# Expert lists loaded ahead of the first weights, four column strips for small last tiles, and the tail's products moved last in a mixture-of-experts kernel

## The chip, the cores and the metric

The kernel runs on one core of a Trainium2 chip. The metric is device time in microseconds (us) of one launch. TensorE (PE in the profile, with PEld for its weight loads) multiplies, VectorE (DVE) and ScalarE (ACT) work on SBUF and PSUM, GpSimd (POOL) issues the indirect transfers (gathers and scatters by a list of indices), and SyncE (SP) issues most of the plain transfers. All arithmetic is float32, and each float32 product leaves two matmul records in the trace.

## What is computed

```python
x = x + xattn(layernorm(x), ctx_2048, ...)      # 8 x 256 tokens of 512, 32 heads, 8 key groups
x = x + ffn(layernorm(x), ...)                  # mixture of experts over the 2048 tokens

def ffn(hidden):                                # T = 2048, H = 512
    logits = x @ gate_w.T                       # 32 experts
    w, sel = top 4 of them, softmax weights normalised to sum 1
    large = sum over chosen e of cw[t,e] * (silu(x @ Wg[e]) * (x @ Wu[e])) @ Wd[e]       # inner width 192
    small = the same with cWg, cWu, cWd of chunk e // 2                                  # inner width 128
    return large + 0.05 * small
```

The reference evaluates all experts for all tokens and masks with `cw`; the kernel evaluates only the chosen pairs, about 4 x 2048 of them.

## The kernel before, in words

**First stage (to about 470 us).** Attention runs over eight batches by a table of slots. Each finished tile of 128 tokens is normalised, its rows are written to `xn_all` in DRAM, its four experts per token are found, and POOL scatters one entry (token number, weight) per choice into `lists` in DRAM, four indirect transfers a tile (L546). The two most loaded experts so far are worked on "ahead" for the first tokens while attention ends.

**Second stage.** Experts are ranked by load on the chip, and rank r gets a fixed capacity `CAPS[r]` (352, 320 x3, 304 x4, 288 x4, 272 x5, 256 x2, 240 x6, 224 x3, 208, 192, 160, 128). The order of work is `RANKS`: first the two smallest (128 and 160), then 352, 320 and so on down to 192. A loop L1285 runs over these 32 shares; what overflows a capacity would go to a loop at the end (L1307), which has nothing to do here. For share i:

- `numbers(i)` (L1198) loads the expert's number and the start of its list into SP registers; for all but the first it is held behind the last weight load recorded so far.
- `fetch_list(i)` (L1209, `list_of` L978) loads the list from DRAM: one transfer of 8-byte entries on SP, and a second of 64 rows if the share's last tile is "few".
- `fetch_weights(i)` (L1218, `weights_of` L965) loads `wm` (1,280 KB) and `sm` (768 KB) on SP; for i = 1 and 2 the load of `wm` also waits until the gathers of i - 1 have landed. Four buffers of each.
- `fetch_tokens(i)` (L1222, `tokens_of` L988) gathers the rows, one indirect transfer on POOL for each 128 tokens; three buffers.
- `turned` (L1008) transposes rows on TensorE into `exT`, four chunks, which stand between the five products of the share before; `inner` (L1025) makes g, u, ug, gs and us (five products of four 128-row steps) and from them the three operands `a`, `at` (64 wide, the tail of the 192) and `b`.
- `down` (L1067) makes the second layer by tiles of 128 tokens, `py`, then evicts them (`evict`, ACT and DVE) and scatters them with add into `out` on POOL (L1091).

`tiles_of` (L999) sorts tiles: full ones by pairs ("first", "second"), a last tile of up to 64 tokens is "few". For a pair the 64-row tail products of the two tiles use the upper and lower half of TensorE's rows at once, and stand between the products of `a` and of `b` (L1121 to L1127). A few tile puts `a` on output partitions 0 to 63 and `b` on 64 to 127, so both run at once, and the two halves are added in the eviction, for which the list's weights are loaded a second time to partitions 64 to 127.

SP and POOL each take their instructions in program order. At the seam between the stages, L1261 to L1284, the order on SP is: number of share 0, `wm` 0, list start of share 0, `sm` 0, numbers of shares 1 and 2, lists 0, 1 and 2, weights 1, weights 2, list 3. A list can be loaded only when all scatters into `lists` have landed. On POOL it is: the last scatters into `lists`, gathers 0 and 1, the add of the first ahead expert (L1248), gathers 2, gathers 3, the add of the second, then the stores of share 0.

Of the kernel before, what the change touches and what calls it, by code (L numbers as in the profile page):

```python
# [10 lines left out]
F32 = mybir.dt.float32  # L11
# [3 lines left out]
ALU = mybir.AluOpType  # L15
AX = mybir.AxisListType

P = 128
B, S, E = 8, 256, 512
# [13 lines left out]
RANKS = [len(CAPS) - 1, len(CAPS) - 2] + list(range(len(CAPS) - 2))  # L33
SHARES = [CAPS[r] for r in RANKS]
NS = (max(CAPS) + P - 1) // P
HALF = P // 2
MAXT = B * S
NO_ONE = NS * P

# [25 lines left out]
def xattn_moe(ctx: ExitStack, tc, x, ctxT, wqT, wkT, wvT, wfcT, bfc, gateT, wx, ws, out):  # L65
# [6 lines left out]
    nc = tc.nc  # L72
# [6 lines left out]
    lists = nc.dram_tensor("lists", (NE * MAXT, 2), F32, kind="Internal").ap()  # L79
# [21 lines left out]
    def counting(name, n, step, per_partition, base=0):  # L101

        i = const.tile([P, n], I32, tag=f"{name}_i", name=f"{name}_i")
        nc.gpsimd.iota(i, [[step, n]], base=base, channel_multiplier=per_partition)
        f = const.tile([P, n], F32, tag=f"{name}_f", name=f"{name}_f")
        nc.vector.tensor_copy(f, i)
        return i, f

    token_i, _ = counting("token", NT, P, 1, NO_ONE)
    _, part_f = counting("part", 1, 0, 1)  # L110
    _, col_f = counting("col", P, 1, 0)
    iota_e = col_f[:, :NE]
    _, base_f = counting("base", NE, MAXT, 0)
# [32 lines left out]
    with ExitStack() as att:  # L146
# [530 lines left out]
        def ahead(n):  # L677
# [45 lines left out]
            def gated_tail():  # L723
                st = steps["sg"][:HALF, 1, :]
                act.activation(st, sums["ug"][HALF:], AF.Silu)
                for j in range(2):
                    tok = slice(j * P, (j + 1) * P)
                    dve.tensor_tensor(
                        at[j * HALF : (j + 1) * HALF, tok], st[:, tok], sums["ug"][:HALF, tok],
                        ALU.mult,  # L730
                    )
# [8 lines left out]
            def second():  # L740
# [4 lines left out]
                for j in range(2):  # L745
                    part = slice(j * HALF, (j + 1) * HALF)
                    pe.matmul(py[j], lhsT=at[part, toks[j]], rhs=wt[part], start=False, stop=False)
# [119 lines left out]
        for s in range(16 * B + LAG + 6):  # L867
            k, i = divmod(s, 8)
# [7 lines left out]
            b, slot = divmod(s, 16)  # L876
# [7 lines left out]
            if s == 10:  # L884

                hold(nc.sync.dma_start(
                    out=lists.rearrange("(e n) c -> e n c", e=NE)[:, :NO_ONE, :], in_=no_one
                ))
                hold(nc.sync.dma_start(
                    out=lists.rearrange("(e n) c -> e n c", e=NE)[:, NO_ONE : NO_ONE + S, :],  # L890
                    in_=no_one[:, :S, :],
                ))
                hold(nc.sync.dma_start(
                    out=xn_all[:NO_ONE, :].rearrange("(j p) r -> p j r", p=P),
                    in_=nothing.unsqueeze(1).to_broadcast([P, NS, E]),
# [28 lines left out]
        count, _, at_rank = ranked("count", first_ones["took"])()  # L924
# [33 lines left out]
    m2 = ctx.enter_context(tc.tile_pool(name="m2", bufs=2, reuse_waits="tile"))  # L958
# [19 lines left out]
    def list_of(entries, n, ns, few=False):  # L978

        li = ls.tile([P, NS + 1, 2], F32, tag="li", name=f"li_{n}")  # L980
        nc.sync.dma_start(out=li[:, :ns, :], in_=entries.rearrange("(j p) c -> p j c", p=P))
        if few:
            nc.sync.dma_start(out=li[HALF:, NS, :], in_=entries[(ns - 1) * P :][:HALF])
        return li
# [14 lines left out]
    def tiles_of(w):  # L999

        sizes = [min(P, w - i) for i in range(0, w, P)]
        lots = ["few" if m <= HALF and len(sizes) > 1 else "" for m in sizes]
        full = lots.count("")
        for j in range(full - full % 2):
            lots[j] = "second" if j % 2 else "first"
        return list(zip(sizes, lots))
# [60 lines left out]
    def down(n, acts, wm, sm, li, weight, w):  # L1067

        a, at, b = acts
        wa, wt, wb = wm[:, 3 * E : 4 * E], wm[:, 4 * E :], sm[:, 2 * E :]  # L1070
        stores = []
        py = {}
        tiles = tiles_of(w)

        def evict(j):
            m, lot = tiles[j]
            y = m6.tile([P, E], F32, tag="y", name=f"y_{n}_{j}")
            if lot == "few":
                y2 = m2.tile([HALF, E], F32, tag="y2", name=f"y2_{n}_{j}")
                nc.scalar.activation(  # L1080
                    y2[:m], py[j][HALF : HALF + m], AF.Copy, scale=li[HALF : HALF + m, NS, 1:2]
                )
                nc.vector.scalar_tensor_tensor(
                    y[:m], py[j][:m], weight(j)[:m], y2[:m], ALU.mult, ALU.add
                )
            elif j % 2:
                nc.vector.tensor_scalar(y[:m], py[j][:m], weight(j)[:m], None, ALU.mult)  # L1087
            else:
                nc.scalar.activation(y[:m], py[j][:m], AF.Copy, scale=weight(j)[:m])  # L1089
            stores.append(  # L1090
                nc.gpsimd.indirect_dma_start(  # L1091
                    out=out,
                    out_offset=bass.IndirectOffsetOnAxis(
                        ap=li[:m, j, 0:1].bitcast(I32), axis=0
                    ),
                    in_=y[:m],
                    in_offset=None,
                    compute_op=ALU.add,
                )
            )  # L1100
        for j, (m, lot) in enumerate(tiles):
            tok = slice(j * P, (j + 1) * P)
            py[j] = ps_y.tile([P, E], F32, tag="py", name=f"py_{n}_{j}")
            if lot == "first":
                continue
            if lot == "few":


                tok = slice(j * P, j * P + HALF)
                nc.tensor.matmul(py[j][:HALF], lhsT=a[:, tok], rhs=wa, start=True, stop=False)  # L1110
                nc.tensor.matmul(py[j][HALF:], lhsT=b[:, tok], rhs=wb, start=True, stop=False)
                for i in range(2):
                    cols = slice(i * (E // 2), (i + 1) * (E // 2))
                    nc.tensor.matmul(
                        py[j][i * HALF : (i + 1) * HALF, cols],
                        lhsT=at[:HALF, tok], rhs=wt[:HALF, cols], start=False, stop=True,
                    )
            else:
                pair = [j - 1, j] if lot == "second" else [j]
                toks = [slice(i * P, (i + 1) * P) for i in pair]  # L1120
                for i, s in zip(pair, toks):  # L1121
                    nc.tensor.matmul(py[i], lhsT=a[:, s], rhs=wa, start=True, stop=False)
                for h, (i, s) in enumerate(zip(pair, toks)):
                    half = slice(h * HALF, (h + 1) * HALF) if len(pair) > 1 else slice(0, P)
                    nc.tensor.matmul(py[i], lhsT=at[half, s], rhs=wt[half], start=False, stop=False)
                for i, s in zip(pair, toks):
                    nc.tensor.matmul(py[i], lhsT=b[:, s], rhs=wb, start=False, stop=True)  # L1127
            for i in [j - 1, j] if lot == "second" else [j]:
                evict(i)
        return stores  # L1130
# [63 lines left out]
    held = {}  # L1194

    loads = []

    def numbers(i):  # L1198


        with tc.issue_after(loads[-1].ins) if i else nullcontext():
            held["expert", i] = nc.sync.value_load(
                order[0:1, RANKS[i] : RANKS[i] + 1], min_val=0, max_val=NE - 1
            )
            held["row", i] = nc.sync.value_load(
                begin[0:1, RANKS[i] : RANKS[i] + 1], min_val=0, max_val=NE * MAXT - NS * P
            )

    def fetch_list(i):  # L1209
        if i < NE:  # L1210
            if i > 2:
                numbers(i)
            held["list", i] = list_of(
                lists[bass.ds(held["row", i], ns_of[i] * P), :], i, ns_of[i],
                tiles_of(SHARES[i])[-1][1] == "few",
            )

    def fetch_weights(i):  # L1218
        if i < NE:
            held["weights", i] = weights_of(held["expert", i], i, gathers.get(i - 1) if i < 3 else None)  # L1220

    def fetch_tokens(i):  # L1222
        if i < NE:
            held["tokens", i] = tokens_of(held["list", i], i, ns_of[i])
# [17 lines left out]
    def behind(instruction):  # L1242
        return tc.issue_after(instruction.ins)
# [14 lines left out]
        ])  # L1258


    numbers(0)  # L1261
    fetch_weights(0)
    for i in range(1, 3):
        numbers(i)
    for i in range(3):
        fetch_list(i)
    fetch_tokens(0)
    fetch_weights(1)
    fetch_tokens(1)
    fetch_weights(2)  # L1270
# [14 lines left out]
    for i in range(NE):  # L1285
# [13 lines left out]
        li = held["list", i]  # L1299
# [7 lines left out]
    with tc.For_i(0, n_extra, 1) as i:  # L1307
        at = line.rearrange("o n c -> o (n c)")
# [4 lines left out]
        li = list_of(lists[bass.ds(row_r, P), :], "l", 1)  # L1313
# [4 lines left out]
        weight = m1.tile([P, 1], F32, tag="weight", name="weight")  # L1318
# [72 lines left out]
```

## Time and profile before

| | us |
|---|---|
| median of 3 runs | 1021.63 (1018.51 to 1031.36) |
| the profiled execution, its own device time | 1017.57 |
| its span, first to last instruction | 1015.4 |
| PE busy | 969.8 |
| DVE, ACT, POOL busy | 410.4, 318.2, 320.6 |
| mean granted TensorE clock | 0.983 |
| first g product of share 0, 1, 2, 3 starts | 497.77, 510.51, 523.52, 544.60 |
| last matmul ends | about 1001 |

By fortieths of the span, PE is at nine tenths or more nearly everywhere, and the row of the moved bytes shows two different halves: below 70 GB/s in most of attention, about 200 GB/s in the experts. Between them lies a short stretch, about 476 to 530 us, in which weights, lists, gathers and scatters of the first shares meet. Times inside the span are given from its start. "Landing" of a transfer is the time at which the trace records its completion.

### The profile page before, as it was taken

To read this page: it belongs to the slowest core of one execution; us is meant where nothing else is said; L and a number is where in the kernel's file an instruction comes from. 1 tells how busy PE (TensorE), PEld (TensorE's weight loads), DVE (VectorE), ACT (ScalarE), POOL (GpSimd) and SP (SyncE) were. 2 spreads that over 40 slices of the span, in tenths; PEclk is the share of its full clock that TensorE was granted. 3 is DMA by queue.
4 is the path that set the end of the run, shared out by engine and by line. 5 is a ranking of instruction groups with operands and counts; after the bars stand their busy time and mean duration, and the time that the engine had idled before them with its cause. 6 is when DMAs were issued, how large, how long until landed. Compare 5 with 4: busy or idle time off the path is not lost. (4 is left out here: it accounts for less than half of the span.)

```text
span 1015.4 us, 13821 instructions
## 1 busy us (share of the span) xinstructions
PE 969.8 (96%) x5068; PEld 594.2 (59%) x5068; DVE 410.4 (40%) x940; ACT 318.2 (31%) x561; POOL 320.6 (32%) x333
## 2 busy tenths in 40 slices
PE   5899999999999999899999999999999999999994
PEld 3445555556565654448665565565657567777773
DVE  4645676667666657535122221222222222122221
ACT  2255554545454544352121111222212111111110
POOL 4200131312222113233336534435343434433322
PEclk9799999999999999999899999999999999999997
DMA  6111010101010000503799876776867577777722
GB/s 219 46 36 65 32 53 33 55 32 34 24 41 12 33 12 33 219 32 92 209 376 190 210 228 176 200 197 180 232 172 223 155 228 229 227 222 213 219 37 33
DMA packets 57510, 133.49 MB, mean 131 GB/s; under 512 B 20737, under 2 KB 26114, under 8 KB 53218
## 3 DMA queue, kind: packets, MB, share of 16 engines
q1 hardware_dynamic: 28050, 79.18, 22.7%
q0 software_dynamic: 18976, 40.25, 19.0%
q10 hardware_dynamic: 10416, 13.18, 3.7%
q8 instruction: 40, 0.66, 0.3%
q14 instruction: 28, 0.23, 0.1%
HBM read 104.76 MB, written 27.56 MB: 130 GB/s over the span
## 5 line engine op out<-in xcount | busy, mean ns | idle before, releaser
L51 DVE TENSOR_REDUCE mx<-sc 128x4 f32<-128x1024 f32 x128 | 156.5, 1223 | 82.2 <-PE st L51 68.5
L51 ACT ACTIVATE pT<-st 128x1024 f32<-128x1024 f32 x128 | 131.0, 1024 | 134.5 <-PE st L51 130.1
L51 PE MATMUL sc<-kT,qT 32*128 32x512 f32 x512 | 146.1, 651 | 9.2 <-DVE mx L51 8.3
L991 POOL DMA_INDIRECT rows<-xn_all,li x80 | 78.7, 983 | 241.1 <-DMA li<-lists 62.2
L51 PE MATMUL st<-qT,k 32*128 32x512 f32 x512 | 144.3, 639 | 3.5 <-DMA qT<-mT 3.5
L1091 POOL DMA_INDIRECT out_dram<-y,li x80 | 122.5, 1531 | 73.7 <-ACT y L1089 45.2
L546 POOL DMA_INDIRECT lists<-ent,slot_i x64 | 62.4, 975 | 117.4 <-DVE slot_i L51 95.1
L1089 ACT ACTIVATE y<-py,li 128x512 f32<-128x512 f32 (+1 forms) x33 | 22.7, 687 | 163.8 <-PE py L1127 163.8
L1087 DVE TENSOR_SCALAR y<-py,li 128x512 f32<-128x512 f32 (+3 forms) x29 | 21.8, 751 | 121.4 <-PE py L1127 121.4
L1021 DVE COPY exT<-ept 128x384 f32<-128x384 f32 (+2 forms) x64 | 31.4, 490 | 94.8 <-PE ept L1015 89.1
L51 PEld LDWEIGHTS sc<-kT,qT 32*128 32x128 f32 x512 | 38.7, 186 | 49.0 <-DVE mx L51 26.4
L51 PE MATMUL pmq<-xT,wq_sb 128*128 128x256 f32 x256 | 63.8, 392 | 1.4 <-ACT xT L51 1.4
L51 PEld LDWEIGHTS pmq<-xT,wq_sb 128*128 128x128 f32 x256 | 46.0, 189 | 30.1 <-issue 23.5
L51 PE MATMUL po<-pT,va 128*32 128x512 f32 x512 | 63.1, 610 | 0.1
L51 PE MATMUL pmf<-wfc_sb,oT 128*128 128x256 f32 x256 | 63.0, 391 | 0.2 <-ACT oT L51 0.2
L1035 PE MATMUL pu_g<-exT,wm 128*128 128x240 f32 (+10 forms) x248 | 62.7, 395 | 0.0
L51 PEld LDWEIGHTS pmf<-wfc_sb,oT 128*128 128x128 f32 x256 | 46.2, 189 | 26.8 <-issue 15.2
L1127 PE MATMUL py<-sm,b 128*128 128x512 f32 x124 | 61.6, 617 | 0.0
L1035 PE MATMUL pu_us<-exT,sm 128*128 128x240 f32 (+10 forms) x248 | 60.6, 387 | 0.0
L1035 PE MATMUL pu_u<-exT,wm 128*128 128x240 f32 (+10 forms) x248 | 60.6, 387 | 0.0
L1035 PE MATMUL pu_ug<-exT,wm 128*128 128x240 f32 (+10 forms) x248 | 60.6, 387 | 0.0
L1035 PE MATMUL pu_gs<-exT,sm 128*128 128x240 f32 (+10 forms) x248 | 60.6, 387 | 0.0
(246 smaller groups left out, 1332.8 us busy)
## 6 DMA issues: line engine op xcount, KB each, us to landing
wm<-in_wx_dram SPq DMA_DIRECT2D x32, 1280.0 KB
sm<-in_ws_dram SPq DMA_DIRECT2D x32, 768.0 KB
acc<-in_x_dram SPq DMA_DIRECT2D x16, 256.0 KB
ctx<-in_ctxT_dram ACTq DMA_DIRECT2D x8, 512.0 KB
out_dram<-acc ACTq DMA_DIRECT2D x16, 256.0 KB
xn_all<-row ACTq DMA_DIRECT2D x16, 256.0 KB
rows<-xn_all,li POOLq DMA_INDIRECT x80, 3.7
out_dram<-y,li POOLq DMA_INDIRECT x80, 8.5
```

Source lines behind the costliest of these rows:

```text
L51: this = instruction(*args, **kwargs)
L546: nc.gpsimd.indirect_dma_start(out=list_views[TOPK * t + k], out_offset=bass.IndirectOffsetOnAxis(ap=slot_i[:, k : k + 1], axis=0), in_=en ...
L991: gathers[n] = nc.gpsimd.indirect_dma_start(out=rows[:, j, :], out_offset=None, in_=xn_all, in_offset=bass.IndirectOffsetOnAxis(ap=li[:, j ...
L1021: nc.vector.tensor_copy(xT[:, kc, : ns * P], pt[:, : ns * P])
L1035: tensor.matmul(pu[:, :w], lhsT=cols(kc), rhs=xT[:, kc, :w], start=(kc == 0), stop=(kc == KC - 1),)
L1087: nc.vector.tensor_scalar(y[:m], py[j][:m], weight(j)[:m], None, ALU.mult)
L1089: nc.scalar.activation(y[:m], py[j][:m], AF.Copy, scale=weight(j)[:m])
L1091: nc.gpsimd.indirect_dma_start(out=out, out_offset=bass.IndirectOffsetOnAxis(ap=li[:m, j, 0:1].bitcast(I32), axis=0), in_=y[:m], in_offset ...
L1127: nc.tensor.matmul(py[i], lhsT=b[:, s], rhs=wb, start=False, stop=True)
```

## The change

```diff
-HALF = P // 2
+HALF, QUARTER = P // 2, P // 4
...
-        lots = ["few" if m <= HALF and len(sizes) > 1 else "" for m in sizes]
+        lots = [
+            "" if m > HALF or len(sizes) == 1 else "few" if m > QUARTER else "very few"
+            for m in sizes
+        ]
...
                 nc.vector.scalar_tensor_tensor(
                     y[:m], py[j][:m], weight(j)[:m], y2[:m], ALU.mult, ALU.add
                 )
+            elif lot == "very few":
+                y2 = m2.tile([QUARTER, E], F32, tag="y2", name=f"y2_{n}_{j}")
+                for q in range(4):
+                    copy = nc.vector.tensor_copy if q % 2 else nc.scalar.copy
+                    copy(y2[:m, q * P : (q + 1) * P], py[j][q * QUARTER :][:m, :P])
+                nc.vector.tensor_scalar(y[:m], y2[:m], weight(j)[:m], None, ALU.mult)
...
+            elif lot == "very few":
+
+                tok = slice(j * P, j * P + QUARTER)
+                for u, w2, of in ((a, wa, P), (b, wb, P), (at, wt, HALF)):
+                    for q in range(4):
+                        nc.tensor.matmul(
+                            py[j][q * QUARTER : (q + 1) * QUARTER, :P],
+                            lhsT=u[:of, tok], rhs=w2[:of, q * P : (q + 1) * P],
+                            start=u is a, stop=u is at,
+                        )
             else:
                 pair = [j - 1, j] if lot == "second" else [j]
                 toks = [slice(i * P, (i + 1) * P) for i in pair]
                 for i, s in zip(pair, toks):
                     nc.tensor.matmul(py[i], lhsT=a[:, s], rhs=wa, start=True, stop=False)
+                for i, s in zip(pair, toks):
+                    nc.tensor.matmul(py[i], lhsT=b[:, s], rhs=wb, start=False, stop=False)
                 for h, (i, s) in enumerate(zip(pair, toks)):
                     half = slice(h * HALF, (h + 1) * HALF) if len(pair) > 1 else slice(0, P)
-                    nc.tensor.matmul(py[i], lhsT=at[half, s], rhs=wt[half], start=False, stop=False)
-                for i, s in zip(pair, toks):
-                    nc.tensor.matmul(py[i], lhsT=b[:, s], rhs=wb, start=False, stop=True)
+                    nc.tensor.matmul(py[i], lhsT=at[half, s], rhs=wt[half], start=False, stop=True)
...
-        with tc.issue_after(loads[-1].ins) if i else nullcontext():
+        with tc.issue_after(loads[-1].ins) if i > 2 else nullcontext():
...
-    numbers(0)
-    fetch_weights(0)
-    for i in range(1, 3):
+    for i in range(3):
         numbers(i)
-    for i in range(3):
         fetch_list(i)
     fetch_tokens(0)
+    with behind(held["lists", 2]):
+        fetch_weights(0)
     fetch_weights(1)
```

Three things are done. On SP the numbers and lists of shares 0, 1 and 2 now come first, and `wm` 0 and `sm` 0 behind them; the order on POOL stays. A last tile of up to 32 tokens becomes "very few": its 512 output columns are cut into four strips of 128, and strip q is written to output partitions 32q to 32q + 31, so that four products of 32 weight columns can stand side by side in TensorE; the strips are put together by two ACT and two DVE copies, and DVE multiplies by the weights. This holds for ten shares: 160, 288 (four) and 272 (five). For them the second list transfer is no longer made. In full tiles the tail's product now comes after that of `b`.

More of the change, by code (lines that the diff above doesn't have):

```diff
@@ L980, in list_of @@
         li = ls.tile([P, NS + 1, 2], F32, tag="li", name=f"li_{n}")
-        nc.sync.dma_start(out=li[:, :ns, :], in_=entries.rearrange("(j p) c -> p j c", p=P))
+        held["lists", n] = nc.sync.dma_start(
+            out=li[:, :ns, :], in_=entries.rearrange("(j p) c -> p j c", p=P)
+        )
         if few:
@@ L1117, in down @@
                     )
+            elif lot == "very few":
[6 more added lines that the diff above has]
+                            start=u is a, stop=u is at,
+                        )
             else:
```

## The prediction, made before the changed kernel ran

> **What bounds the kernel now.** I read the page's busy times, then the windows by stage, then the timeline of PE in one expert and at the seam, then SP's waits. The first lines say where time can be won.
>
> ```profile
> PE 969.8 (96%) x5068; PEld 594.2 (59%) x5068; DVE 410.4 (40%) x940; ACT 318.2 (31%) x561; POOL 320.6 (32%) x333
> ...
> 496.00:500.00 4.00, 2.20 (x15) 1.42 (x12) 1.24 (x3) 1.12 (x4) 3.39 (x3) 0.99 0.94 327
> 500.00:506.00 6.00, 5.33 (x25) 5.33 (x26) 1.26 (x4) 0.65 (x2) 2.24 (x3) 0.50 1.05 332
> 506.00:512.00 6.00, 5.88 (x31) 4.22 (x29) 0.35 (x2) 1.48 (x4) 0.00 (x0) 0.94 1.01 393
> 512.00:514.00 2.00, 0.57 (x3) 0.38 (x4) 0.00 (x0) 0.10 (x1) 0.00 (x0) 1.00 1.13 426
> 514.00:530.00 16.00, 16.00 (x82) 10.96 (x82) 3.86 (x9) 3.87 (x8) 6.28 (x6) 1.00 1.05 373
> ```
>
> The columns are length, PE, PEld, DVE, ACT, POOL, then granted clock, DMA share, GB/s. PE is the bound nearly everywhere; in the windows from 520 to 1000 us it is busy 480 of 480. The exception is the seam: PE half idle at 496 to 500, then half the clock for 6 us, idle again at 512 to 514. From 497 to 530 the DMA share is about 1.
>
> ```profile
> 500.67 0.47 PE L51 MATMUL ept<-ident,rows 128*128 128x128 f32 x1 [1.65 <-DMA rows<-xn_all,li]
> 500.94 1.91 PE L51 MATMUL pu_u<-exT,wm 128*128 128x128 f32 x8
> ...
> 507.04 1.06 PE L51 MATMUL pu_us<-exT,sm 128*128 128x128 f32 x8
> ...
> 512.83 0.33 PE L1015 MATMUL ept<-ident,rows 128*128 128x128 f32 x1 [0.95 <-DMA rows<-xn_all,li]
> 513.76 0.33 PE L1015 MATMUL ept<-ident,rows 128*128 128x128 f32 x1 [0.60 <-DMA rows<-xn_all,li]
> ...
> SPq L981 <- DMA lists<-ent,slot_i: 8.2, 1, 8.2
> ```
>
> PE waits for gathered rows; the same eight matmuls take 1.91 us at half clock and 1.06 at full. Behind that stands SP, which waits 8.2 us for the scatters into `lists`: the last is issued at 479.39 and lands at 488.83, because `wm` 0 and `sm` 0 (2.1 MB, issued at 476.20 and 477.78) are in the way. The scatters at 444 to 455, with no weights beside them, land 2.4 to 3.8 us after their start.
>
> ```profile
> 804.37 1.88 PE L1122 MATMUL py<-wm,a 128*128 128x512 f32 x4
> 806.18 1.13 PE L1125 MATMUL py<-wm,t 64*128 64x512 f32 x4
> 807.24 1.98 PE L1127 MATMUL py<-sm,b 128*128 128x512 f32 x4
> 809.15 0.64 PE L1110 MATMUL py<-wm,a 128*64 128x512 f32 x1
> ...
> 810.16 0.65 PE L1114 MATMUL py<-wm,t 64*64 64x256 f32 x4
> 810.74 0.73 PE L1035 MATMUL pu_g<-exT,wm 128*128 128x272 f32 x2
> ```
>
> This is the second layer of a 272 share. A record of 512 columns steps by 0.429 us (804.370, 804.799). From the last `a` record, 805.657, to the first tail record is 0.523: a change of the array's tiling costs 0.094. Going back to 128*128 also shows the first weight load: the first `b` step is 0.533, so 0.104 more. Records of the two halves (806.180, 806.187) or of four strips (`po` at 442.214, 442.220, 442.227, 442.234) start together.
>
> **Tail last.** For a pair the order tail, `b` became `b`, tail. Followed by a small tile (320 x3, 304 x4, 288 x4, 272 x5: 16 shares), tail to `b` (0.094 + 0.104) disappears and nothing new comes, since the small tile's change was there after `b`: 16 x 0.198 = 3.2 us. Followed by 128*128 work, g or the lone third tile of 352 (13 shares), the same 0.198 returns before it: 0. Lone tiles are 128*128 throughout: 0. What `b` loses is its cover: DVE finishes it at 805.08, and the last `a` ends at 806.09, 1.0 us later, against 0.19 for the weight load. In a lone tile it is 996.97 against 997.21, still just enough; cover gone, it would cost some 0.1 us in each of three shares. The pair's first eviction starts 0.9 us later; the next user of its PSUM buffer comes some 12 us later: 0.
>
> **Four strips.** Before, from the end of `b` (809.06) to g with its bare first load (810.74 + 0.104) is 1.78 us: two steps of 0.429, two of 0.213, the rest changes and first loads. After, six passes of 128 columns, 0.107 each (0.429/4, four strips at once), two first loads of 32 columns (0.027 in `po`: 0.453 against 0.427), three changes and g's load: 0.094 + 0.134 + 3 x 0.107 + 0.094 + 0.134 + 0.107 + 0.094 + 0.104 = 1.08. Saved 0.70 a tile; nine shares after the seam: 6.3 us. [...] `po` shows four strips for the price of one (16 records, 1.92 us, where 4 x 0.429 = 1.72). [...] I take the row, it is the same instruction form; bounds 0.8 saved and 1.2 lost a tile. The eviction: ACT and DVE copies by the 128x128 `exT` copies (0.27 and 0.28, two each) and a DVE multiply from SBUF (0.54, `row`), 1.1 us, against 0.68 + 0.74 before; nothing on PE waits for it (ACT and DVE are 20 to 24% busy there): 0. Ten list transfers of 64 rows fewer: SP and DMA, hidden from share 3 on: 0.
>
> **Lists first.** SP: six register loads and their checks (475.2 to 480.4 before, inside the 8.2 us wait) stay hidden. Then SP waits for the last scatter, now about 483 (479.39 + 3.5); behind this wait stand three list loads, then `wm` 0 and `sm` 0. List 0 goes at 483.0, not 489.09; `wm` 0 at about 485.1, not 476.20; it is needed at 497.77, and two megabytes take 6.4 to 9 us (`wm` 1 and `sm` 1: 496.3 to 505.3 beside gathers), so 495: in time, 2 to 3 us of cover for `wm`, more for `sm`. POOL follows the list by 6.1 us: gathers 0 at 485.6, not 491.69, the ahead adds at 489.4 (their operands are ready at 487.4), gathers 2 at 493.2. PE still ends the ahead work at 496.3. Rows 1 now land near 494 and are there: the 1.65 us wait and the half clock go, and us of share 0 starts at 502.3 (steps of 0.89 + 0.22) instead of 507.04: 4.7 us.
>
> What is late next: rows 2 (22.0 us from gather 0 to the landing at 513.72; 485.6 + 22 + 1 for sharing with `wm` 0 = 508.6, wanted at 507), and then rows 3. List 3 stands on SP's queue behind weights 0, 1, 2, now 6.3 MB from 486.4 instead of 4.2 MB from 496.3. At the 0.257 MB/us of before (496.3 to 512.6) that is 510.9, list 3 1.3 us later, 512.2 against 513.9. Rows 3 landed at 526.11 as PE wanted them (525.99), so they now land 2.1 earlier, 3.3 if the queue speeds up when POOL's part is over. PE is there at about 520 and waits some 3 us. So the seam gives 2.1 to 3.3, not 4.7, and perhaps a half clock: after 3.5 us idle (426.6 to 430.15) the clock was 0.58 over 431 to 435, 1.7 us lost; at 500 to 506 gaps of 1 to 2 us cost 3 us. [...] I take 1.2: 1.5 us.
>
> **Sum.** 3.2 + 6.3 + 1.5 = 11.0 us off the profiled execution's 1017.57 (span 1015.4 and 2.2 around it): 1006.6. The median, 1021.63, is 4.1 above that execution; I add it: 1010.7.
>
> **The rivals.**
> 1. Rows 3 come in time and the seam gives about 5: 1007. For it: POOL's part ends earlier, so SP's queue may run faster; against it, the DMA share of 1 up to 530.
> 2. The seam gives nothing or loses 2 (weights 0 late, or 3 us of half clock): 1012 to 1014.
> 3. Slower: narrow strips do not overlap. Then six passes cost 4 x 0.107 each, a tile 3.0 us, 9 x 1.2 = 11 lost against 4.7 won: 1028. It decides from 0.31 us a pass, where a tile costs 2.3. For it: weights change at every pass and a new load is due every 0.027 us. Against it: loads of `po` start 0.007 us apart.
> 4. The change does not do what it says: the scheduler could undo the orders; but the built orders of SP and PE show them, so only the timing is open.
>
> **Chances.** Main case 0.5; rival 1 0.2; rival 2 0.22; rival 3 and other losses 0.08. The range 1003 to 1018 leaves out rival 3 and the ends of run to run spread. More than 2% faster (under 1001.2) needs rival 1 and more than I can find: 0.05. Beyond 2% slower (over 1042.1): 0.02. Within 2%, about what a measurement here can tell from no change: 0.93.
>
> **What would show it.** List 0 issued near 483 and gathers 0 near 485.6; no wait at the second row transpose, clock 1.0 at 500 to 506; a wait of about 3 us before the first transpose of rows 3 near 520; 272 shares shorter by 0.9 us, 240 shares unchanged; strips starting within 0.03 us of each other. It is wrong if PE waits for `wm` 0, if strips follow each other by 0.1 us, or if PE waits before `b`.

## The result, and the profile after

The changed kernel takes 1011.7 us in the median of 19 runs (1008.14 to 1020.72), where the kernel before, run beside it, takes 1021.57. The ratio is 0.9892, with a 95% interval of 0.9863 to 0.9920 (the ratios here are estimated over the single runs; the quotient of the medians is 0.9903). That is within 2%, and 1 us above the forecast of 1010.7. In most kernels some runs lie 5 to 13 us over the median, at a mean granted clock of 0.968 to 0.975 where the others have 0.978 to 0.987, and the medians include them. The profiled execution took 1009.71 us, with a span of 1007.6. PE's part of the page:

```profile
PE 961.1 (95%) x5228; PEld 595.6 (59%) x5228; DVE 413.9 (41%) x960; ACT 316.1 (31%) x571; POOL 321.2 (32%) x333
```

PE is busy 8.7 us less than before, with 160 instructions more (the strips). DVE has 3.5 us more, and the lengths of the shares below show no wait for it. The seam, by the same windows as before (length, PE, PEld, DVE, ACT, POOL, granted clock, DMA share, GB/s):

```profile
496.00:500.00 4.00, 4.00 (x17) 2.50 (x15) 0.42 (x1) 0.38 (x1) 3.08 (x4) 1.00 1.06 319
500.00:506.00 6.00, 5.17 (x28) 3.16 (x28) 1.51 (x4) 1.50 (x4) 0.83 (x1) 1.00 1.04 371
506.00:512.00 6.00, 6.00 (x42) 4.80 (x41) 1.34 (x5) 1.24 (x4) 0.00 (x0) 1.00 1.00 415
512.00:514.00 2.00, 2.00 (x15) 1.76 (x14) 0.05 (x1) 0.99 (x2) 0.00 (x0) 1.00 1.09 407
514.00:530.00 16.00, 14.12 (x90) 9.87 (x89) 3.60 (x10) 3.12 (x8) 6.03 (x5) 1.00 1.06 374
```

The half clock at 500 to 506 is gone, and so are the waits for rows 1 and 2. That is not yet the work of the lists: PE's ahead work ended 6.5 us later than in the profile of before (the first transpose of rows 0 is at 502.85), so the rows had more time to come. Of these 6.5 us, 2.1 lie before PE counts the last tokens (472.19 and 474.31), ahead of all that the change touches. Another 1.9 us are lost at 520, where `b` of the second expert came late. So the g of the fourth expert starts at 545.91, where it started at 544.60: within this one pair of profiles the seam gave nothing, or 0.8 us if both are counted from the last tokens. Nearly the whole gain lies behind it. SP waits for the scatters into `lists` only for 2.1 us now:

```profile
SPq L981 <- DMA lists<-ent,slot_i: 2.1, 1, 2.1
```

The length of this wait also depends on when SP comes to it: it is 3.4 to 8.2 us in the six profiles below with the weights first and 1.7 to 5.1 in the four with the lists of three shares first. What the edit is for is seen better from POOL's last scatter into `lists` to the first gather of rows 0, before and after:

```profile
479.39 0.96 POOL L546 DMA_INDIRECT lists<-ent,slot_i  x1 [0.30 <-issue]
491.69 0.98 POOL L991 DMA_INDIRECT rows<-xn_all,li  x1 [11.34 <-DMA li<-lists]
...
481.51 0.96 POOL L546 DMA_INDIRECT lists<-ent,slot_i  x1 [0.30 <-issue]
489.07 0.98 POOL L993 DMA_INDIRECT rows<-xn_all,li  x1 [6.61 <-DMA li<-lists]
```

The second layer of a 272 share, to be set beside the lines of before (timeline of PE: start, busy time, line, operation):

```profile
798.28 1.88 PE L1143 MATMUL py<-wm,a 128*128 128x512 f32 x4
800.00 1.88 PE L1145 MATMUL py<-sm,b 128*128 128x512 f32 x4
801.81 1.13 PE L1148 MATMUL py<-wm,t 64*128 64x512 f32 x4
802.87 0.43 PE L1134 MATMUL py<-wm,a 128*32 128x128 f32 x8
803.11 0.40 PE L1134 MATMUL py<-sm,b 128*32 128x128 f32 x8
803.44 0.42 PE L1134 MATMUL py<-wm,t 64*32 64x128 f32 x8
803.80 0.72 PE L1040 MATMUL pu_g<-exT,wm 128*128 128x272 f32 x2
```

`b` follows `a` without a break (records 0.429 apart, 799.572 to 800.001): no change of tiling and no bare load stands between them. The small tile takes 0.93 us (802.87 to 803.80), where it took 1.59 (809.15 to 810.74). From one g to the next, shares have these lengths:

| share | before | changed | difference |
|---|---|---|---|
| 320 (the first; the two others) | 19.07; 18.56 | 18.87; 18.36 | 0.20 |
| 304 | 18.03 | 17.83 | 0.20 |
| 288 | 17.50 | 16.64 | 0.86 |
| 272 | 16.96 | 16.10 | 0.86 |
| 352, the second 256, 240 | 21.07, 14.21, 13.67 | 21.07, 14.21, 13.67 | 0 |

Sixteen shares at 0.20 and nine at 0.66 more make 9.1 us. The whole stretch agrees: from the g of the fourth expert to the end of the last matmul it is 456.08 us before and 446.97 after. (The first 256 share goes from 14.31 to 14.21, and the last share gets 0.10 longer: the bare first load of g now falls one share later.)

### The profile page after: what moved, and what is told of

Same layout as the page of the kernel before. It is cut to its first block, busy times and chain, and to the rows that moved or that the text cites. A ratio compares the mean times of both kernels' runs of the same rounds, so it can differ in the third digit from the quotient of the medians.

```text
span 1007.6 us, 14090 instructions
## 1 busy us (share of the span) xinstructions
PE 961.1 (95%) x5228; PEld 595.6 (59%) x5228; DVE 413.9 (41%) x960; ACT 316.1 (31%) x571; POOL 321.2 (32%) x333
## 5 line engine op out<-in xcount | busy, mean ns | idle before, releaser
L1145 PE MATMUL py<-sm,b 128*128 128x512 f32 x124 | 58.7, 593 | 1.9 <-DVE b L1068 1.9
```

## The experiments

**One part at a time.** The first three kernels carry one part of the change each, the fourth the strips and the tail without the lists. The edits stand against the kernel before; "..." marks what is left out of them.

Lists only:

```
-        with tc.issue_after(loads[-1].ins) if i else nullcontext():
+        with tc.issue_after(loads[-1].ins) if i > 2 else nullcontext():
...
-    numbers(0)
-    fetch_weights(0)
-    for i in range(1, 3):
-        numbers(i)
     for i in range(3):
+        numbers(i)
         fetch_list(i)
     fetch_tokens(0)
+    with behind(held["lists", 2]):
+        fetch_weights(0)
```

> Only the first three lists load ahead of the weights; strips and tail as before. My sum: 1.5 us off, ratio 0.9985 (some 1020.1 where before is 1021.6), with list 0 issued near 483 to 486 instead of 489.1 and rows 1 there when PE wants them. Rival 1 (the seam gives its full 5 us): ratio 0.995. Rival 2 (the seam gives nothing or loses 2): ratio 1.000 to 1.002. If the new gaps of PE between 477 and 484 that the changed kernel's profile shows come from this part, they are here too, and the ahead work ends near 503; if they come from the run, or from the tail or strips, they are gone and it ends near 496.

Strips only (with the eviction of the diff above):

```
+            elif lot == "very few":
+                tok = slice(j * P, j * P + QUARTER)
+                for u, w2, of in ((a, wa, P), (b, wb, P), (at, wt, HALF)):
+                    for q in range(4):
+                        nc.tensor.matmul(
+                            py[j][q * QUARTER : (q + 1) * QUARTER, :P],
+                            lhsT=u[:of, tok], rhs=w2[:of, q * P : (q + 1) * P],
...
```

> Only the four strips of columns for last tiles of up to 32 tokens. My sum: nine shares (288 x4, 272 x5) shorter by 0.70 us each, 6.3 us off, ratio 0.9938; 320 and 304 unchanged. [...] If the strips gained only by coming after a tail that is last (the changing of the array's tiling counted twice in my steps), less than 0.5 each.

Tail only:

```
+                for i, s in zip(pair, toks):
+                    nc.tensor.matmul(py[i], lhsT=b[:, s], rhs=wb, start=False, stop=False)
                 for h, (i, s) in enumerate(zip(pair, toks)):
...
-                for i, s in zip(pair, toks):
-                    nc.tensor.matmul(py[i], lhsT=b[:, s], rhs=wb, start=False, stop=True)
```

> Only the order of a pair: a, b, tail. My sum: 16 shares (320, 304, 288, 272) shorter by 0.198 us each, 3.2 us off, ratio 0.9969; 352, 256, 240, 224, 208 unchanged. If a bare wait for b at DVE ate it, 0.1 or less each, and lines of py from b would show idle time before them, also in large shares. If the saving were in every pair, 256 and 240 would be 0.2 shorter too, some 2.4 us more.

Strips and tail, which is the last two edits together:

> The changed kernel without its first part: weights of the first expert load ahead of the lists again. If the parts add up, 9.5 us off, ratio 0.9907, and the changed kernel (0.9892) owes 1.5 us to the lists. If the lists cost what one profile of the changed kernel shows (g of the third expert 1.3 us later than before), this is as fast or faster than the changed kernel: 0.988 to 0.9893. If the lists give 5, this stands at 0.994.

| kernel | median, us | ratio to before | interval | 320 / 288 / 272 share |
|---|---|---|---|---|
| before, same chip | 1018.84 | | | |
| lists only | 1017.46 | 0.9969 | 0.9940 to 0.9998 | 19.07 / 17.50 / 16.96 |
| strips only | 1012.07 | 0.9931 | 0.9920 to 0.9943 | 19.07 / 16.83 / 16.30 |
| tail only | 1015.80 | 0.9979 | 0.9952 to 1.0006 | 18.87 / 17.30 / 16.76 |
| strips and tail | 1008.90 | 0.9920 | 0.9890 to 0.9949 | 18.87 / 16.64 / 16.10 |

Times are compared on one chip only: the kernel before has 1018.84 here and 1021.57 beside the result. The strips alone save 0.66 us in every 288 and 272 share, the tail alone 0.20 in those and in 320 and 304, and both together the sum, 0.86. From the g of the fourth expert to the last matmul it is 450.13 us with the strips, 452.92 with the tail, 446.97 with both, where before and the lists alone have 456.08: 5.95 and 3.16 make 9.11. Nothing was counted twice, and 352 and 240 do not move in any of them. In time the strips give 6.8 us of median and the tail 3.0; the interval of the tail alone holds 1, so its gain rests on the share lengths. For the lists the intervals are too wide to tell 1.5 from 5.

What the lists do to the seam is seen in the timelines of PE. With the lists alone:

```profile
513.66 0.33 PE L1017 MATMUL ept<-ident,rows 128*128 128x128 f32 x1 [3.39 <-DMA rows<-xn_all,li]
...
527.96 0.33 PE L1017 MATMUL ept<-ident,rows 128*128 128x128 f32 x1 [1.49 <-DMA rows<-xn_all,li]
```

And with the strips and the tail, weights first again:

```profile
511.16 0.30 PE L1018 MATMUL ept<-ident,rows 128*128 128x128 f32 x1 [2.40 <-DMA rows<-xn_all,li]
512.85 0.33 PE L1018 MATMUL ept<-ident,rows 128*128 128x128 f32 x1 [1.39 <-DMA rows<-xn_all,li]
513.83 0.47 PE L1018 MATMUL ept<-ident,rows 128*128 128x128 f32 x1 [0.65 <-DMA rows<-xn_all,li]
```

PE waits for rows 2 till nearly the same moment, 513.7 and 513.8, though SP issued the lists first in one and the weights first in the other. But the last scatter into `lists` is at 482.40 in the first and at 481.11 in the second; counted from it, rows 2 came 31.3 and 32.7 us later. The pauses of PE at 477 to 484 that the changed kernel's profile had are in none of these four.

**The changed kernel, and the one with strips and tail, again on one chip.**

> The changed kernel once more, for its seam. If the pauses of PE between 477 and 484 and the one before the products with b of the second expert (1.88 us at 522.00) belong to the change, they stand here again. If they are pauses of one execution (ACT and DVE both stood still), they are gone: the ahead work then ends 4 us earlier against pm_order, and by my sum a wait of 1.5 to 3 us stands before the first transpose of rows 3 instead. Time as before, 1008 to 1012.

> Strips and tail without the lists, on the same chip as the changed kernel. My sum has it 1.5 us above the changed kernel; rival 1 5 us above; rival 2 equal or up to 2 us below. The rows of the third expert came at 513.3 to 513.9 in all profiles, with the lists first or not, so I now expect 0 to 1.5 above.

Before: 1021.51. Changed: 1010.10, ratio 0.9896 (0.9860 to 0.9931). Strips and tail: 1012.61, ratio 0.9919 (0.9895 to 0.9944). So the lists are worth 2.5 us here as a difference of medians, more than the 0 to 1.5 that I had come to expect, with intervals that overlap. The pauses at 477 to 484 stand in both profiles, with the lists first (1.72 and 1.09 us) and without (1.76 and 1.81): they do not belong to the lists. The pause before `b` is gone from the changed kernel and stands in the other (2.01 us, up to 523.13). Where it is gone, the wait that I had forecast for rows 3 appears (timeline of PE in the changed kernel's second profile):

```profile
525.22 0.33 PE L1020 MATMUL ept<-ident,rows 128*128 128x128 f32 x1 [1.00 <-DMA rows<-xn_all,li]
527.04 0.47 PE L1020 MATMUL ept<-ident,rows 128*128 128x128 f32 x1 [1.49 <-DMA rows<-xn_all,li]
```

**What holds rows 3.** In the next kernel list 3 is loaded ahead of the weights as well; in the one after it, gathers 2 also go ahead of the first ahead adds in POOL's queue.

```
-        with tc.issue_after(loads[-1].ins) if i > 2 else nullcontext():
+        with tc.issue_after(loads[-1].ins) if i > 3 else nullcontext():
...
+    fetch_list(3)
     fetch_tokens(0)
-    with behind(held["lists", 2]):
+    with behind(held["lists", 3]):
         fetch_weights(0)
...
-    fetch_list(3)
```

> The changed kernel with list 3 ahead of the weights too. If list 3 behind the weights of three experts is what holds rows 3 (it came at 513.0, gathers 3 went at 514.30), gathers 3 now go at about 502 to 504, when rows 0 are done with, the wait before the first transpose of rows 3 is gone, and the fourth expert's g comes 1 to 2.5 us earlier against pm_order: ratio to the kernel before 0.987 to 0.988. Rival: the queues are full from 490 to 530, so the 0.8 MB of rows 3 only push out rows 2 or weights 1 and 2: no gain, or 1 to 2 us lost at the rows or weights of the third expert.

> As the one with list 3 first, and gathers 2 ahead of the first ahead adds. If the adds in POOL's queue hold rows 2, which came at 513.3 to 513.9 in every profile, those now land 3 us or more earlier, no wait is left before the transposes of rows 2 and 3, and the seam gives 2 to 4 us more than in the changed kernel: ratio 0.985 to 0.987. If the rate of the queues holds them, rows 2 land at about 513 again and nothing is won.

The first gather of rows 3 on POOL's timeline, in the changed kernel:

```profile
514.30 0.94 POOL L993 DMA_INDIRECT rows<-xn_all,li  x1 [13.47 <-PE ept L1020]
```

and with list 3 first:

```profile
504.75 0.94 POOL L993 DMA_INDIRECT rows<-xn_all,li  x1 [3.94 <-PE ept L51]
```

The name behind the arrow has to be read with care in the first of them. The gather waits for two things: list 3, and the end of PE's transposes of rows 0, whose buffer it takes. The second line shows when the buffer comes free: with the list there, the gather goes at 504.75. In the changed kernel those transposes are over at about the same time, so the other 9.5 us are the wait for list 3, whose packets ran from 511.8 to 513.0, behind six weight transfers on SP's queue. With list 3 first, PE has no wait for rows 2 or rows 3, and the third expert's share takes 21.07 us where the changed kernel's second profile has 25.34. That alone would not settle it, since the changed kernel's first profile has 21.07 too, with a pause in the wait's place, and this one has a pause as well; the two profiles of the next kernel, also with list 3 first, have no pause between g of the first share and g of the fourth and no wait either. The median is 1008.79, ratio 0.9879 (0.9849 to 0.9908), against 1010.10 for the changed kernel beside it.

The g of the fourth expert comes 71.4 us after the counting of the last tokens (71.6 and 72.2 in the changed kernel), with a pause of 1.70 before `b` in the first share, where PE waits for DVE and not for rows; so of the 1 to 2.5 us expected only 0.2 to 0.8 show.

The second edit on top of it:

```
     with behind(gathers[1]):
-        add_ahead(0)
-    with behind(before[-1]):
         fetch_tokens(2)
     with behind(gathers[2]):
+        add_ahead(0)
+    with behind(before[-1]):
         fetch_tokens(3)
```

With gathers 2 moved too, the first three shares take 8.01, 10.35 and 21.07: no wait for any row is left there. It was timed twice.

> List 3 first too, and gathers 2 ahead of the first ahead adds, timed again: 1006 to 1009 where before is 1021.5, ratio 0.985 to 0.988; no wait for rows 2 or rows 3 in the seam, g to g of the first three shares 8.01, 10.35 and 21.07 but for pauses of ACT and DVE. If the earlier run's 0.9889 holds and the changed kernel stands at 0.989, the order of the queues behind the seam is worth nothing that can be measured.

Medians are 1009.64 and 1008.67, ratios 0.9889 (0.9845 to 0.9933) and 0.9886 (0.9839 to 0.9932). Both its profiles have a stretch of half clock from about 443 to 467, ahead of all that the edit touches, so their spans (1015.5 and 1015.9) say nothing of it; from the counting to g of the fourth expert they take 69.7 and 71.1. That is 0.5 to 2.5 us below the changed kernel's two profiles, where I had expected 2 to 4, and the intervals do not separate its times from the changed kernel's: what the order of the queues wins in the seam is too little to be told by these runs. Since list 3 alone already took the waits away, these runs cannot tell whether the adds had held rows 2.

**One strip instead of four.** The price of my third rival, with one pass of 512 columns where four of 128 stand side by side, and one copy in the eviction:

```
-                for q in range(4):
-                    copy = nc.vector.tensor_copy if q % 2 else nc.scalar.copy
-                    copy(y2[:m, q * P : (q + 1) * P], py[j][q * QUARTER :][:m, :P])
+                nc.scalar.copy(y2[:m], py[j][:m])
...
-                    for q in range(4):
-                        nc.tensor.matmul(
-                            py[j][q * QUARTER : (q + 1) * QUARTER, :P],
-                            lhsT=u[:of, tok], rhs=w2[:of, q * P : (q + 1) * P],
-                            start=u is a, stop=u is at,
-                        )
+                    nc.tensor.matmul(
+                        py[j][:QUARTER], lhsT=u[:of, tok], rhs=w2[:of],
+                        start=u is a, stop=u is at,
+                    )
```

> The changed kernel with last tiles of up to 32 tokens in one strip of 512 columns, the other three strips of the array empty: what my rival 3 would have made of four strips that do not overlap. Six passes of 0.429 in place of six of 0.107, two first loads and two changes as before: the 272 shares 1.9 us longer than in the changed kernel (some 18.5 and 18.0 in place of 16.63 and 16.10), nine shares 17 us, ratio to the kernel before 1.006, so slower than before. [...]

The median is 1027.27 where before is 1021.02, ratio 1.0056 (1.0031 to 1.0080). The 288 and 272 shares take 18.52 and 17.98, each 1.88 longer than with four strips. The small tile of one of them:

```profile
818.75 1.04 PE L1131 MATMUL py<-wm,a 128*32 128x512 f32 x2
819.63 1.02 PE L1131 MATMUL py<-sm,b 128*32 128x512 f32 x2
820.58 1.04 PE L1131 MATMUL py<-wm,t 64*32 64x512 f32 x2
821.55 0.73 PE L1040 MATMUL pu_g<-exT,wm 128*128 128x272 f32 x2
```

It takes 2.81 us against 0.93, for the same products. The rival's mechanism and its price are right; what it needs, strips that follow one another, does not occur. This is also what narrow tiles cost when only one strip of the array is used: slower than before, where the tile took 1.59.

**The kernel before again, for the pauses.**

> The kernel before once more, for its seam: whether the pauses of ACT and DVE between 477 and 484 (2.8 to 3.6 us of PE idle in four profiles, none in four others) come with the kernel or with the run. If with the run, they may stand here too; g of the fourth expert at 72 to 75 us after the counting of the last tokens, shares from the fourth on as in the first profile to 0.02.

Timeline of DVE, ACT and PE:

```profile
480.50 0.42 DVE L51 COPY xT_ahead<-pmt_ahead 128x256 f32<-128x256 f32 x1
...
481.26 1.13 PE L51 MATMUL pm_ahead_g<-xT_ahead,up_ahead 128*128 128x256 f32 x4 [0.67 <-ACT xT_ahead L51]
...
483.67 0.42 DVE L51 COPY xT_ahead<-pmt_ahead 128x256 f32<-128x256 f32 x1 [2.74 <-PE pm_ahead_g L51]
483.72 0.37 ACT L51 COPY xT_ahead<-pmt_ahead 128x256 f32<-128x256 f32 x1 [2.51 <-PE pm_ahead_g L51]
...
484.15 2.08 PE L51 MATMUL pm_ahead_g<-xT_ahead,up_ahead 128*128 128x256 f32 x4 [1.75 <-DVE xT_ahead L51]
```

The pauses are in the kernel before as well, so they do not come from the change. DVE stands for 2.7 us and ACT for 2.5, though the transposes that they copy ended before 479; PE then waits 1.75 for the copies. The time was 1019.50, and the seam starts as in the changed kernel: first transpose of rows 0 late, no half clock at 500 to 506, first share 8.01 us. What I had read in the first profile there, 12.74 for that share, is not the rule: of the six profiles with the weights first, one other has a long first share (strips only, 10.98), and four have 8.0 to 8.2.

The prediction had named a wait of PE before `b` as a sign of being wrong. In the steady shares there is none, but in the seam it came, as here in the changed kernel's first profile (timeline):

```profile
521.62 0.32 DVE L1068 SCALAR_TENSOR_TENSOR b<-ss,pu_us 128x160 f32<-128x160 f32 x1 [3.98 <-remote]
...
522.00 1.12 PE L1145 MATMUL py<-sm,b 128*128 128x512 f32 x2 [1.88 <-DVE b L1068]
```

In five of the thirteen profiles, all of them with the pauses above, DVE starts `b` 1.5 to 2.5 us after the us product has ended, in one of the first two shares, against 0.1 elsewhere. This profile of the kernel before is one of them (1.83 late, in the second share), but there the tail's product stands ahead of `b`, and PE idles for only 0.49; with the tail last it idles for 0.98 to 2.01. Of the delay 1.34 us are covered there (1.83 - 0.49) and 0.48 in the lines above, where `b` is 2.36 late (2.36 - 1.88), so in a lone tile the tail had hidden 0.86 us of it, which the new order gives up. In all five POOL is at work on the adds of an ahead expert while `b` is late; but three profiles on another chip have these adds at the same place and no late `b`, so the cause is not shown.

## Why the forecast came true, and where it didn't

**The tail: right.** 0.198 a share was forecast in 16 shares, and 0.20 was measured in just these (19.07 to 18.87, 18.56 to 18.36, 18.03 to 17.83 and, with the tail alone, 17.50 to 17.30 and 16.96 to 16.76), none in the others. The lone tiles' lost cover for `b`, for which I had named 0.1 us, costs nothing where `b` is on time (352: 21.07 before and after); where it is late, as in the seam above, it costs up to 0.86.

**The strips: right, a size a little off.** Forecast 0.70 a tile, measured 0.66. The six passes start at 802.870, 803.004, 803.113, 803.222, 803.444 and 803.578, and g at 803.797. The step with a first load, 0.134, is as forecast, and a plain step is 0.109 for 0.107. The term that is off is the change of tiling: between passes of 128 columns a step with a change is 0.222 or 0.219, of which 0.113 and 0.110 are the change, not the 0.094 that I had taken from steps of 0.523 between long passes (the one-strip kernel has 0.523 there again). Two such changes make up 0.035 of the 0.04. The row that I had gone by, that of `po`, held for strips of 128 columns too: the four start 0.007 us apart, as there, and the pass takes 0.109 where a quarter of 0.429 is 0.107.

**The lists: sum right within what can be measured, the working not.** To compare seams across runs I take the time from PE's counting of the last tokens, which all of this follows, to g of the fourth expert:

| kernel | weights first | lists first |
|---|---|---|
| before, twice | 72.4, 72.6 | |
| strips; tail; both, twice | 73.1; 73.0; 71.4, 75.3 | |
| changed, twice | | 71.6, 72.2 |
| lists only | | 71.2 |
| mean | 73.0 | 71.7 |

The lists give 1.3 us by this mean, where I had 1.5; profiles of one kernel lie up to 4 us apart, and by medians the lists give 1.4 and 2.5. Profiles with and without the pauses of ACT and DVE are mixed here; set apart, both kinds point the same way (without: 72.5 and 71.2, with: 74.0 and 71.9). Rival 1 (5 us) would need seams of 68, which none shows. That the sum came out is in part luck, since three steps of my working fell.

- List 0 was to go near 483 and gathers 0 at 485.6. They went at 486.39 and 489.07. I had the last scatter at 479.39, from one profile; here POOL issues it at 481.51, and it takes 4.9 us from there to list 0. From the last scatter to gathers 0 it is 9.8 to 12.3 us in the six profiles with the weights first and 7.1 to 7.7 in the four with the lists of three shares first (means 11.0 and 7.4; the one with one strip is the fourth): the edit wins 3.6 us there, not 6.1. That the weights stand in the way of the scatters was right.
- The wait and the half clock at 500 to 506 were to go and give 4.7 us. They were there to be taken in two of the six profiles with the weights first (a wait of 1.65 us in the first of before, of 1.21 with the strips alone) and not in the second of before. In the one profile with the lists first and no pauses, that of the lists alone, they are gone as forecast, but PE then waits 3.39 us for rows 2, where my working had 1.6.
- Rows 3 were to land 2 to 3 us earlier. List 3's packets ended at 513.0 in the changed kernel and 513.45 in the kernel before, and gathers 3 went at 514.30 and 514.67. Counted from the last scatter, gathers 3 go 33.6 to 35.3 us after it in the six profiles with the weights first and 32.5 to 34.5 in the four with the lists first: 1.0 us earlier in the mean. In the changed kernel's second profile PE waits for rows 3 for 2.5 us, and half a clock follows, as I had it. In its first profile the pause before `b` used up that time instead. The 1.2 us for a half clock there, which I had taken off the middle of 2.1 to 3.3, were my estimate, and no run shows them: in the second profile the half clock cost 1.8 us, and with the lists alone, where PE waits 1.49 us for rows 3, the clock stayed at 1.00.

List 3 on SP's queue as the next thing that is late was the right name: loading it first took the wait away, and the third share's 25.34 us became 21.07, which is its length wherever nothing waits. Of those 4.3 us, 2.5 were the waits and 1.8 the slower clock behind them.

**The sum.** 9.1 us by the shares behind the seam, 1.3 by the seam: 10.4 of the forecast 11.0, and the medians differ by 9.9. The 9.1 are shown share by share; the 1.3 are a mean over profiles that scatter by more than that. What stays open is why ACT and DVE pause, and why `b` is late in some seams.

## What to carry to other kernels

A small last tile that leaves most of the array's columns empty is worth splitting into column strips: four strips of 128 columns took 0.109 us for what one strip does in 0.429. Sort work so that a change of the array's tiling stands where another change comes anyway; each pair of them was worth 0.2 us here, in all 16 shares where a small tile follows and in no other. Work out a transfer-bound seam from more than one profile: its waits moved by several us between runs of the same kernel, while the steady loops repeated to 0.02 us. And count its times from an event that the change leaves alone: the whole seam shifted by 2 us between two profiles.

## What the runs showed of the hardware that was not expected

- **Pauses of ACT and DVE.** In eight of the thirteen profiles ACT and DVE stand together for 1 to 3 us once or more while the last ahead work runs, with their operands long made, and PE loses 2.5 to 3.6 us there, where the other five have one gap of 0.44. None of the four profiles taken on one chip has them, all seven taken on two other chips do, and the kernel before has them in one profile and not in the other. The rows name PE's products, which in the lines above had ended 1.3 us before the copies start (481.26 + 1.13); what the engines wait for is not shown.
- **The clock after short gaps.** In these profiles the length of a gap does not tell what it costs. One gap of 1.88 us left the clock at 1.00, and so did one of 3.39 us with the lists alone; one of 2.01 us (strips and tail, second profile) and two of together 2.5 us within 2.8 (changed kernel, second profile) each brought it to half for 3.4 us. In the changed kernel's first profile:

```profile
520.00:522.00 2.00, 0.12 (x2) 0.01 (x1) 0.32 (x1) 0.67 (x2) 1.55 (x1) 1.00 1.02 419
522.00:526.00 4.00, 4.00 (x32) 2.05 (x33) 0.41 (x2) 1.20 (x3) 0.00 (x0) 1.00 1.09 330
```

and in its second:

```profile
524.00:527.00 3.00, 0.55 (x3) 0.14 (x1) 0.77 (x2) 0.72 (x2) 0.00 (x0) 0.90 1.15 265
527.00:530.00 3.00, 2.96 (x6) 1.89 (x7) 0.56 (x1) 0.00 (x0) 0.00 (x0) 0.53 1.10 393
```

In the first profiles of the kernel before and of the changed kernel the recorded clock is 1.00 or 0.50 and changes only at whole steps of 3.41 us. In all thirteen profiles together it falls to 0.50 thirteen times between 470 and 540 us, each time for 3.4 or 6.8 us. In the 3.41 us ahead of such a fall PE had been busy for 1.73 (kernel before, fall at 499.88), 1.63 (changed kernel's first profile, 484.18), 1.57 (its second) and 1.40 (strips and tail, second profile); with the gap of 1.88 it was 1.79, and the clock stayed at 1.00. It stayed there also over the gap of 3.39 with the lists alone, so what decides a fall is not shown. What one cost is: a wait of together 2.5 us made the third share 4.3 us longer (25.34 for 21.07).
